# Attention rows: x and kv transposed by DMA blocks and DVE instead of TensorE, group norm folded into two weights, v and the variances on ScalarE

## The chip, the cores and the metric

The kernel runs on one core of a Trainium2 chip. Its time is that of one execution on the device in microseconds (us). A core has TensorE (PE; PEld is its weight load), VectorE (DVE), ScalarE (ACT), GpSimd (POOL) and the DMA engines; SyncE (SP) issues most of the DMAs. SBUF is the on-chip memory, PSUM the memory that PE writes to, in banks of 512 floats per partition.

## The reference, cut to what matters

Two layers are added to x, of shape (1, 256, 256, 128). The change lies in layer 0: attention along each of the 256 rows, with 4 heads of 32 channels, on a group-normalised x.

```python
# layer 0: x = x + L0(_gn(x), kv_x, ...)      _gn: 32 groups of 4 channels over the whole image, eps 1e-5
q = split_heads(einsum('...qi,oi->...qo', q_x, wq)) / sqrt(32)
k = split_heads(einsum('...ki,oi->...ko', kv_x, wk))
v = split_heads(einsum('...ki,oi->...ko', kv_x, wv))
a = softmax(einsum('bshqd,bshkd->bshqk', q, k) + bias1 + bias2, axis=-1)
o = einsum('bshqk,bshkd->bshqd', a, v)
g = sigmoid(einsum('...qi,oi->...qo', q_x, wg) + bg)
out = einsum('...qi,oi->...qo', o * g, wo) + bo
# layer 1: x = x + L1(_gn(x), ...)   tokens = channels; instance norms, small Fourier modes, mixing
```

bias1 is (head, query, key) and the same for all rows; bias2 is (row, key). Everything is float32.

## The kernel before, in words

`layer0` first streams the whole of x for the group statistics (xb, L135 to L140), meanwhile turns the weights, and ends with the mean and the scale of each channel (mr, nmr). `Rows.prepare` makes exp(bias1), scaled, with keys on partitions (b1T), and bias2 with keys on partitions (b2T).

Then `Rows.run` goes over the 256 rows, one row of 256 tokens by 128 channels an iteration. The order on PE, ACT, DVE and POOL is the order in which the code is written (`tc.manual_schedule`); only SP's order is left to the scheduler. Each engine works through its own list and waits where an input or a buffer is not ready. Iteration i holds the steps of several rows:

- `load` (L242, every second iteration): x and kv of two rows, tokens on partitions, two neighbouring tokens to a partition.
- `scores(i)` (L305): eight matmuls of 32 channels, into two PSUM tiles of two banks each, s0 and s1, with one buffer each. Then three of the four exps on ACT (L314), with bias2 as the bias column: those of heads 0 and 1 stay in PSUM (sc), those of heads 2 and 3 go to e1 in SBUF.
- `project(i+1)`: q and k (L279, L280), copied by ACT to qkT (L282); v and the gate (L285, L289), v copied by DVE (L291), the gate through tanh on ACT (L293). The fourth exp of row i follows.
- `turn(i+2)`: four 128x128 transposes of x and kv on PE (L268, L269), then two ACT steps to SBUF: the group norm applied to x (xnT, L271) and a copy of kv (kvT, L273).
- `weigh(i)`: DVE multiplies heads 0 and 1 by b1T out of PSUM (e0, L327), POOL heads 2 and 3 in SBUF (e1, L332); then POOL adds the two key halves of each pair of heads (es, L336, twice), which is half of the softmax's sum.
- `out(i-3)`: the output projection (L366), the sum with x1 on DVE (L370), the store to x1d.
- `spectrum(i-4)`: x1 turned on PE (L379) and its Fourier sums over the row (L381); DVE takes bn_stats of the turned row (L384), ACT copies the sums (L385).
- `attend(i-1)`: e times v and the sums of es over keys, both into one bank (L344, L349); DVE: og = (gate + 1) times that (L355), a reciprocal of the sums (L356), their product (L357); POOL: x + bo (L360).

PSUM tiles other than the scores share one pool of four banks under tag "a", taken in turn: qk, gv, tr, wo, u, av each iteration. A step that takes a bank waits for the readers of the tile that had it four tiles earlier.

A few one-time steps stand in DVE's list: in iterations 8 to 15 a reduce over b1T each (L413), in iteration 16 five tiny steps on the results (L419 to L423), and every 32 rows `gather`, which sums up the bn_stats. They decide whether the biases are small enough; if not, `layer0_general` does the rows again, which does not happen with these inputs.

Of the kernel before, what the change touches and what calls it, by code (L numbers as in the profile page):

```python
# [18 lines left out]
P = 128  # L19
# [50 lines left out]
class Groups:  # L70
# [13 lines left out]
    def make(self, pool, psum, mv2, tag):  # L84

        nc = self.nc
        mv = pool.tile([P, 2], FP, name=tag + "mv")
        dv = pool.tile([P, 8], FP, name=tag + "dv")
        nc.vector.tensor_reduce(mv[:, 0:1], mv2[:, :, 0], AX.X, ALU.add)
        nc.vector.tensor_scalar(mv[:, 0:1], mv[:, 0:1], 0.125, None, ALU.mult)  # L90
        nc.vector.tensor_scalar(dv, mv2[:, :, 0], mv[:, 0:1], None, ALU.subtract)
        nc.vector.tensor_mul(dv, dv, dv)
        nc.vector.tensor_add(dv, dv, mv2[:, :, 1])
        nc.vector.tensor_reduce(mv[:, 1:2], dv, AX.X, ALU.add)
        nc.vector.tensor_scalar(mv[:, 1:2], mv[:, 1:2], 0.125, None, ALU.mult)
        nc.vector.tensor_copy(self.mr, group_stats(nc, pool, psum, mv, self.gavg, tag))
        nc.vector.tensor_scalar(self.bdft, self.raw, self.mr[:, 1:2], None, ALU.mult)


def layer0(tc, I, C, ident, x1d, U, stats2, mv2, groups):  # L100
# [11 lines left out]
    with ExitStack() as ctx:  # L112
# [4 lines left out]
        nmr = const.tile([P, 1], FP, name="nmr1")  # L117
        bg = const.tile([P, 1], FP, name="bg")

        bad = const.tile([P, 3, 8], FP, name="bad")  # L120
# [4 lines left out]
        rows = Rows(tc, I, rctx, x1d, U, stats2, mv2, wT, mr, nmr, bg, adft, bad, ident)  # L125
        with tc.tile_pool(name="l0p", bufs=2) as pp, tc.tile_pool(
# [6 lines left out]
            for b in range(xr.shape[0]):  # L133
# [7 lines left out]
                if b == 2:  # L141
                    nc.sync.dma_start(gavg, C["gavg"])
                    nc.sync.dma_start(bg, I["L0_conv_bg"].unsqueeze(1))
                    nc.sync.dma_start(adft, C["adft"].rearrange("(p j) f -> p j f", j=2))
# [18 lines left out]
            nc.vector.tensor_scalar(nmr, mr[:, 0:1], mr[:, 1:2], -1.0, ALU.mult, ALU.mult)  # L163
# [4 lines left out]
        with tc.tile_pool(name="l0f", bufs=1) as fp, tc.tile_pool(  # L168
# [5 lines left out]
            nc.vector.tensor_scalar(z, bad[:, 2, :], 0.0, None, ALU.mult)  # L174
# [12 lines left out]
            with tc.If(again > 0):  # L187
                layer0_general(tc, I, ident, x1d, U, stats2, wT, mr, bg, adft)
                for k in range(8):
                    nc.vector.bn_aggr(mv2[:, k, :], stats2[:, 32 * k : 32 * k + 32, :].rearrange("p a b -> p (a b)"))  # L190
                groups.make(fp, ps_g, mv2, "g3")


class Rows:
# [6 lines left out]
    def __init__(self, tc, I, ctx, x1d, U, stats2, mv2, wT, mr, nmr, bg, adft, bad, ident):  # L201
        self.tc, self.I, self.ctx, self.x1d, self.U, self.stats2 = tc, I, ctx, x1d, U, stats2
        self.wT, self.mr, self.nmr, self.bg, self.adft = wT, mr, nmr, bg, adft
# [4 lines left out]
        self.ld = ctx.enter_context(tc.tile_pool(name="l0ld", bufs=2))  # L208
        self.hbg = const.tile([P, 1], FP, name="hbg")
        self.bo = const.tile([P, P], FP, name="bo")  # L210
# [5 lines left out]

    def prepare(self, bp, ps_b):
        nc, I, ident = self.tc.nc, self.I, self.ident
        nc.gpsimd.memset(self.ones, 1.0)
        nc.scalar.mul(self.hbg, self.bg, 0.5)  # L220
# [3 lines left out]
        nc.sync.dma_start(b1n, I["L0_conv_bias1"][0, 0].rearrange("h (p j) k -> p h j k", j=2))  # L224
        b2n = bp.tile([P, 2, 256], FP, name="b2n", bufs=1)
        nc.sync.dma_start(b2n, I["L0_conv_bias2"][0, :, 0, 0, :].rearrange("(j p) k -> p j k", p=P))
        for h in range(4):
            ps = ps_b.tile([P, 512], FP, tag="a", name=f"b1ps_{h}")
            for c in range(2):
                for j in range(2):  # L230
                    nc.tensor.transpose(
                        ps[:, (2 * c + j) * P : (2 * c + j + 1) * P], b1n[:, h, j, c::2], ident
                    )
# [4 lines left out]
        for c in range(2):  # L238
            for j in range(2):
                nc.tensor.transpose(  # L240
                    ps[:, (2 * c + j) * P : (2 * c + j + 1) * P], b2n[:, j, c::2], ident
# [3 lines left out]
    def load(self, g):  # L245
        nc, SG = self.tc.nc, self.SG
        s0 = g * SG
        xt = self.ld.tile([P, SG, 2, P], FP, tag="xt", name=f"xt_{g}", bufs=4)
        nc.sync.dma_start(xt, self.x[s0 : s0 + SG].rearrange("s (p j) c -> p s j c", j=2))
        kt = self.ld.tile([P, SG, 2, P], FP, tag="kt", name=f"kt_{g}")  # L250
        nc.sync.dma_start(kt, self.kv[s0 : s0 + SG].rearrange("s (p j) c -> p s j c", j=2))
        for i in range(SG):
            self.rows[s0 + i] = {"x": xt[:, i], "kv": kt[:, i]}

    def run(self):
# [8 lines left out]
        def turn(s):  # L264
            r = rows[s]
            ps = ps_a.tile([P, 512], FP, tag="a", name=f"tr_{s}")
            for j in range(2):
                nc.tensor.transpose(ps[:, j * P : (j + 1) * P], r["x"][:, j, :], ident)  # L268
                nc.tensor.transpose(ps[:, 256 + j * P : 256 + (j + 1) * P], r["kv"][:, j, :], ident)  # L269
            r["xnT"] = wk.tile([P, 256], FP, tag="xnT", name=f"xnT_{s}")  # L270
            nc.scalar.activation(r["xnT"], ps[:, 0:256], AF.Identity, bias=self.nmr, scale=self.mr[:, 1:2])  # L271
            r["kvT"] = wk.tile([P, 256], FP, tag="kvT", name=f"kvT_{s}")
            nc.scalar.copy(r["kvT"], ps[:, 256:512])  # L273

        def project(s):
            r = rows[s]
            xnT, kvT = r["xnT"], r["kvT"]
            ps = ps_a.tile([P, 512], FP, tag="a", name=f"qk_{s}")
            nc.tensor.matmul(ps[:, 0:256], wT["wq"], xnT, start=True, stop=True)  # L279
            nc.tensor.matmul(ps[:, 256:512], wT["wk"], kvT, start=True, stop=True)  # L280
            r["qkT"] = wk.tile([P, 512], FP, tag="qkT", name=f"qkT_{s}")
            nc.scalar.copy(r["qkT"], ps)  # L282
# [6 lines left out]
            nc.tensor.matmul(ps[:, 0:256], wT["wg"], xnT, start=True, stop=True)  # L289
            r["v"] = wk.tile([P, 2, P], FP, tag="v", name=f"v_{s}", bufs=3)  # L290
            nc.vector.tensor_copy(r["v"].rearrange("p c d -> p (c d)"), ps[:, 256:512])  # L291
            r["gate"] = wk.tile([P, 256], FP, tag="gate", name=f"gate_{s}", bufs=3)
            nc.scalar.activation(r["gate"], ps[:, 0:256], AF.Tanh, bias=self.hbg, scale=0.5)  # L293
            if s > 0:
                rows[s - 1].pop("exp")(1, 1)

        def scores(s):
# [22 lines left out]
            exp(1, 0)  # L320
# [3 lines left out]
        def weigh(s):  # L324
# [9 lines left out]
            for hp in (1, 0):  # L334
                e = r["e"][hp]
                nc.gpsimd.tensor_tensor(r["es"][hp], e[:, :, 0, :], e[:, :, 1, :], ALU.add)  # L336
# [25 lines left out]
        def out(s):  # L362
# [10 lines left out]
            nc.sync.dma_start(self.x1d[s].rearrange("(p j) c -> p j c", j=2), r["x1"])  # L373

        def spectrum(s):
# [8 lines left out]
            nc.vector.bn_stats(self.stats2[:, s, :], ps[:, 0:256])  # L384
            nc.scalar.copy(self.U[:, :, s], ps[:, 256 : 256 + 129])  # L385

        def gather(k):


            st = self.stats2[:, 32 * k : 32 * k + 32, :].rearrange("p a b -> p (a b)")  # L390
            nc.vector.bn_aggr(self.mv2[:, k, :], st)
            nc.vector.tensor_reduce(bad[:, 2, k : k + 1], st, AX.X, ALU.add)

        with tc.manual_schedule(engines={ENG.PE, ENG.Activation, ENG.DVE, ENG.Pool}):
            turn(0)
            turn(1)
            project(0)
            for i in range(NS + 4):
                if i % SG == 0 and i // SG + 2 < NS // SG:
                    self.load(i // SG + 2)  # L400
                if i < NS:
                    scores(i)
                if i + 1 < NS:
                    project(i + 1)
                elif i < NS:
                    rows[i].pop("exp")(1, 1)
                if i + 2 < NS:
                    turn(i + 2)
                if i < NS:
                    weigh(i)  # L410
# [13 lines left out]
                if i % 32 == 7 and i > 32:  # L424
                    gather(i // 32 - 1)
# [7 lines left out]
            gather(7)  # L433


def layer0_general(tc, I, ident, x1d, U, stats2, wT, mr, bg, adft):
# [4 lines left out]
    with ExitStack() as ctx:  # L441
# [5 lines left out]
        nc.sync.dma_start(b1, I["L0_conv_bias1"][0, 0].rearrange("h (p j) k -> p h j k", j=2))  # L447
# [4 lines left out]
        with tc.For_i(0, NS, 1) as s:  # L452
            one = bass.ds(s, 1)
            xt = wk.tile([P, 2, P], FP, name="g_xt")
            nc.sync.dma_start(xt, x[one].rearrange("s (p j) c -> p (s j) c", j=2))
# [78 lines left out]
            nc.sync.dma_start(x1d[one].rearrange("s (p j) c -> p (s j) c", j=2), x1)  # L534
# [7 lines left out]
            nc.vector.bn_stats(stats2[:, one, :].rearrange("p o k -> p (o k)"), ps[:, 0:256])  # L542
# [3 lines left out]
def layer1(tc, I, C, ident, x1d, upool, U, stats2, groups, out):  # L546
# [1547 lines left out]
```

## Time and profile before

| | |
|---|---|
| timed runs | 2865.82, 2868.55, 2876.69 us; median 2868.55 |
| profiled execution, first to last instruction (the only time the page has of it) | 2861.4 us |
| PE busy | 2629.8 us, 92% |
| DVE busy | 2008.6 us, 70% |
| POOL busy | 1668.0 us, 58% |
| ACT busy | 1488.9 us, 52% |
| statistics of x | until about 108 us |
| attention rows | about 110 to 1652 us |
| layer 1 | the rest |
| DMA packets | 245121, 424.35 MB |
| granted clock of PE, mean | 0.958 (1.00 in the rows) |

The profile is one execution. Busy time is that of instructions that do work, not of waits. In a list by time each line is a start in us, a length in us, the engine, the line of the kernel, the operation, output<-inputs by the program's tile names, the shape and how many instructions were merged; square brackets hold the idle time before it and what ended that. In the table of stretches, busy time of each engine (and its instructions) is followed by PE's granted clock, the DMA engines' mean busy share and GB/s.

### The profile page before, as it was taken

How to read it: one execution, taken by the hardware profiler on the slowest of the kernel's cores; microseconds unless marked ns; L12 is line 12 of the kernel's file. 1: busy time of each engine (PE TensorE's matmuls, PEld its weight loads, DVE VectorE, ACT ScalarE, POOL GpSimd, SP SyncE). 2: the span in 40 equal slices, each digit the busy share in tenths (PEclk: the TensorE clock that was granted, in tenths of full speed). 3: DMA queues.
4: the chain of work that ended last, by engine and by line, in shares of the span. 5: the costliest groups of instructions: out<-in, count | busy, mean ns of one | idle time of the engine just before them, and what ended most of it. 6: DMA issues, size and time to landing. Idle time of an engine off the chain costs nothing. (4 is left out here: it accounts for less than half of the span.)

```text
span 2861.4 us, 71473 instructions
## 1 busy us (share of the span) xinstructions
PE 2629.8 (92%) x29116; PEld 1922.9 (67%) x29116; DVE 2008.6 (70%) x3274; ACT 1488.9 (52%) x2847; POOL 1668.0 (58%) x1298
## 2 busy tenths in 40 slices
PE   6799999999999999999999989999897988789655
PEld 6677777777777777777777755778675555545433
DVE  7788888888888888888888853756664656356445
ACT  0477777777777777777777721310103621355132
POOL 0399999999999999999999900300214632111211
PEclk9999999999999999999999999999998999899855
DMA  9422222222222222222222101088887784898599
GB/s 367 171 68 68 68 68 67 67 68 68 68 68 68 68 68 68 67 65 65 65 66 68 53 28 54 1 272 274 291 296 266 253 301 141 278 350 303 189 357 345
DMA packets 245121, 424.35 MB, mean 148 GB/s; under 512 B 26102, under 2 KB 174025, under 8 KB 238392
## 3 DMA queue, kind: packets, MB, share of 16 engines
q1 hardware_dynamic: 204984, 329.57, 34.7%
q0 software_dynamic: 22912, 81.80, 7.4%
q10 hardware_dynamic: 16896, 8.39, 1.0%
q8 instruction: 231, 3.78, 0.6%
q14 instruction: 98, 0.80, 0.1%
HBM read 284.40 MB, written 135.27 MB: 147 GB/s over the span
## 5 line engine op out<-in xcount | busy, mean ns | idle before, releaser
L332 POOL TENSOR_TENSOR e<-e,b1T 128x1024 f32<-128x1024 f32 x256 | 606.7, 2370 | 163.7 <-PE u L381 88.8
L336 POOL TENSOR_TENSOR es<-e 128x512 f32<-128x512 f32 x512 | 639.9, 1271 | 20.1
L314 ACT ACTIVATE sc<-sc,b2T 128x512 f32<-128x512 f32 x512 | 339.0, 662 | 364.6 <-PE sc L305 356.3
L356 DVE RECIPROCAL av<-av 128x256 f32<-128x256 f32 x256 | 452.3, 1767 | 27.2 <-DVE og L355 1.4
L314 ACT ACTIVATE e<-sc,b2T 128x512 f32<-128x512 f32 x512 | 348.7, 681 | 0.0
L327 DVE TENSOR_TENSOR e<-sc,b1T 128x1024 f32<-128x1024 f32 x256 | 311.1, 1215 | 0.0
L305 PE MATMUL sc<-qkT 32*128 32x256 f32 x4096 | 293.4, 400 | 1.3 <-DVE e L327 1.3
L344 PE MATMUL av<-e,v 128*32 128x256 f32 x4096 | 274.7, 385 | 0.5 <-POOL e L332 0.5
L1352 PE MATMUL yps<-xt,mpT 128*128 128x256 f32 x1024 | 247.4, 392 | 28.3 <-DVE yt L1364 14.4
L305 PEld LDWEIGHTS sc<-qkT 32*128 32x128 f32 x4096 | 185.1, 184 | 112.3 <-issue 97.8
L355 DVE SCALAR_TENSOR_TENSOR og<-gate,av 128x256 f32<-128x256 f32 x256 | 107.8, 421 | 190.6 <-PE av L349 190.6
L1352 PEld LDWEIGHTS yps<-xt,mpT 128*128 128x128 f32 x1024 | 192.6, 193 | 72.7 <-DVE yt L1364 19.9
L1368 POOL DMA_DIRECT2D yd<-yt x32 | 17.5, 546 | 314.6 <-DVE yt L1364 311.9
L360 POOL TENSOR_TENSOR x<-xt,bo 128x256 f32<-128x256 f32 x256 | 188.1, 735 | 0.0
L279 PE MATMUL qk<-xnT,wT_wq 128*128 128x256 f32 x512 | 179.5, 432 | 1.7 <-ACT xnT L271 1.7
L285 PEld LDWEIGHTS gv<-wT_wv,kvT 128*128 128x128 f32 x1024 | 155.0, 192 | 13.4
L349 PE MATMUL av<-es,ones 128*32 128x256 f32 x2048 | 157.5, 379 | 2.6 <-POOL es L336 2.5
L366 PE MATMUL wo<-wT_wo,og 128*128 128x128 f32 x1024 | 156.8, 276 | 2.7 <-DVE og L357 2.7
L344 PEld LDWEIGHTS av<-e,v 128*32 128x32 f32 x4096 | 107.0, 109 | 76.1 <-POOL e L332 1.0
L381 PE MATMUL u<-adft,x 128*128 128x129 f32 x1024 | 156.4, 275 | 0.0
L291 DVE COPY v<-gv 128x256 f32<-128x256 f32 x256 | 108.7, 425 | 67.5 <-PE gv L289 67.5
L285 PE MATMUL gv<-wT_wv,kvT 128*128 128x128 f32 x1024 | 156.0, 275 | 0.0
(543 smaller groups left out, 5228.5 us busy)
## 6 DMA issues: line engine op xcount, KB each, us to landing
xt<-x1d SPq DMA_DIRECT2D x128, 512.0 KB, 6.7
xb<-in_x_dram SPq DMA_DIRECT2D x32, 1024.0 KB, 7.8
xt<-in_x_dram SPq DMA_DIRECT2D x128, 256.0 KB, 2.7
kt<-in_L_conv_kv_x_dram SPq DMA_DIRECT2D x128, 256.0 KB
x1d<-x SPq DMA_DIRECT2D x256, 128.0 KB, 2.6
y<-yd SPq DMA_DIRECT2D x62, 512.0 KB, 7.3
gs<-Gd SPq DMA_DIRECT2D x384, 64.0 KB, 5.4
yd<-yt POOLq DMA_DIRECT2D x32, 512.0 KB, 6.2
```

The costliest lines, as they stand in the source:

```text
L279: nc.tensor.matmul(ps[:, 0:256], wT["wq"], xnT, start=True, stop=True)
L285: nc.tensor.matmul(ps[:, 256 + c * P : 256 + (c + 1) * P], kvT[:, c * P : (c + 1) * P], wT["wv"], start=True, stop=True,)
L305: nc.tensor.matmul(sc[h // 2][:, h % 2, c * 256 : (c + 1) * 256], qkT[p, 256 + c * P : 256 + (c + 1) * P], qkT[p, 0:256], start=True, stop ...
L314: nc.scalar.activation(r["e"][1][:, :, c, :] if hp else z, z, AF.Exp, bias=b2T[:, c, s : s + 1])
L327: nc.vector.tensor_tensor(r["e"][0].rearrange("p h c q -> p (h c q)"), r.pop("sc").rearrange("p h x -> p (h x)"), b1T[:, 0:2].rearrange("p ...
L332: nc.gpsimd.tensor_tensor(e1, e1, b1T[:, 2:4].rearrange("p h c q -> p (h c q)"), ALU.mult)
L336: nc.gpsimd.tensor_tensor(r["es"][hp], e[:, :, 0, :], e[:, :, 1, :], ALU.add)
L344: nc.tensor.matmul(ps[hd, 0:256], r["v"][:, c, hd], r["e"][h // 2][:, h % 2, c, :], start=(c == 0), stop=(c == 1),)
L349: nc.tensor.matmul(ps[32 * h : 32 * h + 32, 256:512], self.ones, r["es"][h // 2][:, h % 2, :], start=True, stop=True,)
L356: nc.vector.reciprocal(rd, rd)
L360: nc.gpsimd.tensor_tensor(r["x1"], r["x"], bc(self.bo, 1, 2), ALU.add)
L1352: nc.tensor.matmul(rows_of(ps[j]), mpT[:, sc, tt], by_turn(xt[:, sc])[:, j], start=(sc == 0), stop=False,)
```

## The change

In the rows, PE no longer turns x and kv. `load` brings each row twice over: once in blocks, so that partition 32a + t holds channels 32a to 32a+31 of the tokens t, 32 + t, 64 + t and so on, by eight DMAs for two rows (four blocks of channels for x, four for kv), in pieces of 32 floats; and, in the new `load_x`, x with tokens on partitions for the residual. `turn` is one DVE instruction that transposes all 32x32 blocks of x and kv of a row (xkT). The group norm is no longer applied to x: `fold` multiplies wq and wg by the scale once and turns the mean into bias columns (qb for q, hbg for the gate), so qkT becomes an ACT step with a bias. ACT takes over v's copy from DVE, and the row's sum of squares (Square with an accumulator, into Q2) replaces bn_stats; the row sums come from U. The last two exps move behind qkT (`rest`), `weigh` goes ahead of `turn`, and of heads 0 and 1 the es add of head 0 goes to DVE, that of head 1 stays on POOL as a half, ahead of the es add of heads 2 and 3. Tokens 0 to 127 and 128 to 255 of a row now form the two halves where neighbouring tokens were paired, in every layout that depends on it. The PSUM pool has no tr tile any more.

```diff
+def row_sums(nc, U, Q2, mv2, k):
+    t = slice(32 * k, 32 * k + 32)
+    nc.vector.tensor_reduce(mv2[:, k, 0:1], U[:, 0, t], AX.X, ALU.add)
+    nc.vector.tensor_reduce(mv2[:, k, 1:2], Q2[:, t], AX.X, ALU.add)
...
+    def fold(self, psum, mr):
+        nc = self.tc.nc
+        nc.vector.tensor_scalar(self.nm, mr[:, 0:1], -1.0, None, ALU.mult)
+        ps = psum.tile([P, 512], FP, tag="a", name="foldps")
+        for k, n in enumerate(("wq", "wg")):
+            nc.vector.tensor_scalar(self.wn[n], self.wT[n], mr[:, 1:2], None, ALU.mult)
+            nc.tensor.matmul(ps[:, k : k + 1], self.wn[n], self.nm, start=True, stop=True)
+        nc.vector.tensor_copy(self.qb, ps[:, 0:1])
+        nc.vector.tensor_scalar(self.hbg, ps[:, 1:2], self.bg, 0.5, ALU.add, ALU.mult)
...
     def load(self, g):
-        xt = self.ld.tile([P, SG, 2, P], FP, tag="xt", name=f"xt_{g}", bufs=4)
-        nc.sync.dma_start(xt, self.x[s0 : s0 + SG].rearrange("s (p j) c -> p s j c", j=2))
-        kt = self.ld.tile([P, SG, 2, P], FP, tag="kt", name=f"kt_{g}")
-        nc.sync.dma_start(kt, self.kv[s0 : s0 + SG].rearrange("s (p j) c -> p s j c", j=2))
+        t = self.ld.tile([P, 2, 8 * SG, 32], FP, tag="xk", name=f"xk_{g}")
+        for k, src in enumerate((self.x, self.kv)):
+            blocks = src[rs].rearrange("s (b t) c -> t (s b) c", t=32)
+            for a in range(4):
+                ch = slice(32 * a, 32 * a + 32)
+                nc.sync.dma_start(t[ch, k], blocks[:, :, ch])
...
+    def load_x(self, g):
+        xt = self.ld.tile([P, SG, 2, P], FP, tag="xt", name=f"xt_{g}", bufs=2)
+        nc.sync.dma_start(xt, self.x[g * SG : (g + 1) * SG].rearrange("s (j p) c -> p s j c", p=P))
...
         def turn(s):
-            ps = ps_a.tile([P, 512], FP, tag="a", name=f"tr_{s}")
-            for j in range(2):
-                nc.tensor.transpose(ps[:, j * P : (j + 1) * P], r["x"][:, j, :], ident)
-                nc.tensor.transpose(ps[:, 256 + j * P : 256 + (j + 1) * P], r["kv"][:, j, :], ident)
-            nc.scalar.activation(r["xnT"], ps[:, 0:256], AF.Identity, bias=self.nmr, scale=self.mr[:, 1:2])
-            nc.scalar.copy(r["kvT"], ps[:, 256:512])
+            r["xkT"] = wk.tile([P, 512], FP, tag="xkT", name=f"xkT_{s}")
+            nc.vector.transpose(r["xkT"].rearrange("p (k n) -> p k n", k=2), r.pop("xk").rearrange("p k b c -> p k (b c)"))
...
         def project(s):
-            nc.scalar.copy(r["qkT"], ps)
+            nc.scalar.activation(r["qkT"], ps, AF.Identity, bias=self.qb)
+            if s > 0:
+                rest(s - 1)
...
-            nc.vector.tensor_copy(r["v"].rearrange("p c d -> p (c d)"), ps[:, 256:512])
+            nc.scalar.copy(r["v"].rearrange("p c d -> p (c d)"), ps[:, 256:512])
...
-            if s > 0:
-                rows[s - 1].pop("exp")(1, 1)
+        def rest(s):
+            exp = rows[s].pop("exp")
+            exp(1, 0)
+            exp(1, 1)
...
         def weigh(s):
-            for hp in (1, 0):
-                e = r["e"][hp]
-                nc.gpsimd.tensor_tensor(r["es"][hp], e[:, :, 0, :], e[:, :, 1, :], ALU.add)
+            e = r["e"][0]
+            nc.vector.tensor_tensor(r["es"][0][:, 0], e[:, 0, 0], e[:, 0, 1], ALU.add)
+            nc.gpsimd.tensor_tensor(r["es"][0][:, 1], e[:, 1, 0], e[:, 1, 1], ALU.add)
+            e = r["e"][1]
+            nc.gpsimd.tensor_tensor(r["es"][1], e[:, :, 0, :], e[:, :, 1, :], ALU.add)
...
         def spectrum(s):
-            nc.vector.bn_stats(self.stats2[:, s, :], ps[:, 0:256])
+            nc.scalar.activation(
+                ps[:, 0:256], ps[:, 0:256], AF.Square, accum_out=self.Q2[:, s : s + 1]
+            )
...
             for i in range(NS + 4):
+                if i % SG == 1 and i // SG + 1 < NS // SG:
+                    self.load_x(i // SG + 1)
...
+                if i < NS:
+                    weigh(i)
                 if i + 2 < NS:
                     turn(i + 2)
-                if i < NS:
-                    weigh(i)
```

Layer 1's first steps read the row sums in U and Q2 where they read the fields of bn_stats before; a few small DVE steps fall away there.

## The prediction

> **What bounds the kernel now.** I read the page's busy shares first, then the busy table of a stretch in the attention rows, then the order in time inside one row, then the waits.
>
> ```profile
> PE 2629.8 (92%) x29116; PEld 1922.9 (67%) x29116; DVE 2008.6 (70%) x3274; ACT 1488.9 (52%) x2847; POOL 1668.0 (58%) x1298
> ```
>
> ```profile
> 1000.00:1200.00 200.00, 200.00 (x2127) 152.46 (x2127) 162.56 (x237) 149.86 (x301) 185.70 (x134) 1.00 0.21 66
> ```
>
> The second fence is the busy table of 200 us of the row loop (columns PE, PEld, DVE, ACT, POOL, granted clock, DMA share, GB/s). PE has no idle time, at full clock; POOL is at 93%, DVE 81%, ACT 75%; DMA is at 21%. The row loop runs from about 110 to 1650 us; the change lives there.
>
> ```profile
> 1004.64 1.15 PE L305 MATMUL sc<-qkT 32*128 32x256 f32 x16
> 1004.78 0.42 DVE L355 SCALAR_TENSOR_TENSOR og<-gate,av 128x256 f32<-128x256 f32 x1 [0.79 <-PE av L349]
> 1005.30 1.77 DVE L356 RECIPROCAL av<-av 128x256 f32<-128x256 f32 x1
> 1005.88 1.36 ACT L314 ACTIVATE sc<-sc,b2T 128x512 f32<-128x512 f32 x2 [1.47 <-PE sc L305]
> 1007.11 0.42 DVE L357 SCALAR_TENSOR_TENSOR og<-av,og 128x256 f32<-128x256 f32 x1
> 1007.16 0.68 ACT L314 ACTIVATE e<-sc,b2T 128x512 f32<-128x512 f32 x1
> 1007.56 0.27 PE L268 MATMUL tr<-ident,xt 128*128 128x128 f32 x1
> ...
> 1007.73 0.59 ACT L282 COPY qkT<-qk 128x512 f32<-128x512 f32 x1
> ...
> 1008.00 0.61 PE L366 MATMUL wo<-wT_wo,og 128*128 128x128 f32 x4
> 1008.11 1.22 DVE L327 TENSOR_TENSOR e<-sc,b1T 128x1024 f32<-128x1024 f32 x1
> ...
> 1008.45 0.38 PE L379 MATMUL u<-ident,x 128*128 128x128 f32 x2
> 1009.36 2.37 POOL L332 TENSOR_TENSOR e<-e,b1T 128x1024 f32<-128x1024 f32 x1 [0.35 <-PE u L381]
> ...
> 1010.64 1.15 PE L305 MATMUL sc<-qkT 32*128 32x256 f32 x16
> ```
>
> One row, scores to scores, is 1010.64 - 1004.64 = 6.00 us, and PE's starts follow each other without a wait. DVE and ACT wait for PE each row (0.79 and 1.47 us). So today a row is PE's issue time.
>
> **What is removed.** The four transposes of x and kv (L268, L269) hold PE from 1007.56 to 1008.00: 0.44 us. Nothing replaces them on PE, so PE's row becomes 5.56 us. Over about 254 rows that is -112 us, if PE still sets the pace.
>
> **The other engines, busy time per row** (33.3 rows in the 200 us). ACT is 149.86/33.3 = 4.50; it loses xnT 0.57 and kvT 0.38, gains the v copy (kvT's row, 0.38), a Square with accumulator (nearest row L1080, 0.50) and about 0.08 because qkT becomes an ACTIVATE with a bias column (L314 steps 0.57, the COPY 0.49): 4.5. POOL is 5.57; one es add of 1.27 shrinks to half, 0.61 to 0.86 (128x256 adds of L1417): about 5.0. DVE is 4.88; it loses the v copy and bn_stats (0.42 each), gains a 128x256 add (0.42, L370's size) and the 32x32 transpose of 128x512, which no row shows. A COPY of 128x512 from PSUM is 0.69 (L939), from SBUF 0.58 (L769); POOL's slower 128x512 add, 1.27, is my upper bound. I take 0.69, the same size on the same engine: DVE 5.15. All stay under 5.56, so on counts alone the change wins.
>
> The Trainium skill, "VectorE: DVE Perf Modes", section "The three transpose paths", gives 311 ns for a 128x128 transpose on this engine; four of them would be 1.24 us (an estimate), and no run here shows one. By that figure DVE's round worked out below would be 5.74 instead of 5.19 and the blocked rhythm 6.73 us a row.
>
> **Transfers.** Per two rows x and kv come as 8 DMAs of 512 packets of 128 B, plus one x load and two stores in 512 B packets: 4096 + 1024 packets. The row "q10 hardware_dynamic: 16896, 8.39, 1.0%" gives 0.010 x 2861 x 16 / 16896 = 27 ns for a packet of about 500 B. At that price 5120 x 27 / 16 = 8.6 us per two rows, under 11.1; smaller packets should not cost more. At the stretch's 1 KB price (0.204 x 200 x 16 / 13587 = 48 ns) the 128 B ones alone would take 12.3. I take the first: hidden. SP issues 11 DMAs instead of 4 per two rows, 0.4 us each by its rows, 4.6 us of 11.1; in the changed program's order a row's blocks are issued beside the store of the row ten earlier, some four rows ahead of their use, so a landing of 2.7 us is covered. If that cover goes, DVE's transpose waits and all of DVE's row queues behind it.
>
> **The wait that the change adds.** The new es half on DVE is a tensor_tensor with both inputs in SBUF, and POOL is nearly always inside a tensor_tensor. No DVE step of the row loop before is of that kind (each has an input in PSUM), but a one-time step of row 16 is:
>
> ```profile
> 210.06 2.37 POOL L332 TENSOR_TENSOR e<-e,b1T 128x1024 f32<-128x1024 f32 x1 [0.36 <-PE u L381]
> ...
> 210.19 0.15 DVE L422 TENSOR_SCALAR bad<-bad 128x1 f32<-128x1 f32 x1
> 210.38 2.06 DVE L423 TENSOR_TENSOR bad<-bad 128x1 f32<-128x1 f32 x1
> ```
>
> The second view is that of one line of layer 1 (min, median and max in ns):
>
> ```profile
> L1103 DVE SCALAR_TENSOR_TENSOR mT<-pT,hq,mT x7: 744/1482/1487, 1792.7 to 1848.4; 128x512 f32<-128x512 f32 x7
> ```
>
> L423 multiplies two columns, normally 0.15 us, and took until 212.44, the end of POOL's instruction (212.43). L1103, also all SBUF, doubles in the same way when POOL is first. So the price of the new add is 0.42, or the rest of POOL's instruction and then some 0.2.
>
> The Trainium skill says so as a rule against such a change ("SBUF — State Buffer", section "Who interferes with whom"): the DVE instruction with two SBUF inputs and a GpSimd instruction that reads SBUF exclude each other for a whole instruction. By the rule the sum is the one by the row; it also leaves the transpose free if that runs in no two-port mode, which nothing here shows.
>
> So the question is which comes first in a row, counted from the start of scores. POOL's e1 multiply starts after the fourth exp: 1.24 (scores to first exp) + 1.28 (two exps) + 0.57 (qkT, now ahead of the last two) + 0.58 + 0.68 + 0.08 = 4.43. DVE: og at 0.14, reciprocal 0.66, og2 2.47, e0 multiply 2.81, done 4.02, add asked for at 4.06. POOL's previous work ends near 3.8. The add slips in, 0.37 us ahead of e1. DVE's round is then 0.525 + 1.80 + 0.34 + 1.25 + 0.34 + 0.60 + 0.33 = 5.19 (starts to next starts; transpose 0.69 less 0.09 overlap), 0.37 less than PE's 5.56; on every second row seven DMA waits ahead of the transpose may take 0.25 of that.
>
> But rows 8 to 15 carry an extra reduce of 0.676 on DVE (L413; 0.60 in a queue). DVE's round becomes 5.79, 0.23 over PE's, more on the even rows. After two rows the 0.37 is used up, the add finds e1 running and waits to its end at 4.43 + 2.33 = 6.76. Behind it on DVE queue the transpose, the x1 add, og, reciprocal and og2; og2 frees the PSUM bank that the u transposes of the next row on PE need. That closes a loop of two rows: 6.76 + 0.22 (add) + 0.60 + 0.33 + 0.525 + 1.80 + 0.425 + 0.07 (signal), then on PE from u to the next scores 0.76 + 0.89 + 0.55 = 2.20. Sum 12.93 us, **6.46 us per row**. In this rhythm the add is asked for about 0.9 us inside a 2.37 us multiply, so a small jitter does not end it. With a transpose of 0.58 or 1.27 the row is 6.40 or 6.75.
>
> **Small edits.** fold adds a few 0.15 to 0.23 us steps and two matmuls before the first row, layer 1's start loses as many, the moment sums replace bn_aggr: within 2 us together. Plain halves instead of interleaved rows alter no count of work on the engines.
>
> **Sum.** Span 2861.4 us; the median of the runs is 2868.55, 7.1 more, which I keep. About 246 rows at +0.46 = +113, the first eight at -0.44 = -4, rows 8 to 17 some +3 more: 2868.6 + 112 = 2980.
>
> **Rivals.**
> (1) *PE keeps the pace*: the add keeps slipping in ahead of e1 (margin 0.37), or a shift in row 16 restores that order. For it: the counts, PE's unbroken issue. Against it: rows 8 to 15. 2868.6 - 112 = 2757; with 0.02 us a row lost either way 2750 to 2790. It decides as long as DVE lags PE by less than that margin. Chance 0.33.
> (2) *Transfers set the pace*: if a 128 B packet cost the 48 ns of a 1 KB one, two rows need 12.3 + 1.7 (1024 of 27 ns) = 14.0 us, 7.0 a row, +256 us: 3125. It decides from about 36 ns a packet on, where two rows reach 11.1. Against it: the 27 ns row. 0.05.
> (3) *A mix*: stretches of both rhythms, or a multiply that misses by less: 2800 to 2950; a part of this is no change. 0.08.
> (4) *The change does not do what it says*: the transposes stay on DVE at over 1.27 us; then DVE's round is past 5.8 without any lock and the lock only adds: above 3050. 0.05.
> The forecast, add behind e1, 0.49 with its own range 2945 to 3050.
>
> Two in ten may lie outside, so the range must take in both rhythms: 2750 to 3050. Half a per cent, 14 us, is about what a measurement of this kernel tells from no change. Slower by over that: forecast 0.49, transfers 0.05, slow transpose 0.05, a third of the mix 0.03, in all 0.62. Faster: rival 1 with 0.33 and a little of the mix, 0.34. Same: 0.04.
>
> **What would show it.** The es add on DVE near 1.5 to 2.5 us mean instead of 0.42; scores starting 6.4 to 6.5 us apart after row 10 and 5.56 before row 8; PE idle before u, released by DVE; POOL idle before e1. I am wrong if the es add stays near 0.42 (rival 1 then), if DVE waits for xk landings (rival 2), or if the transpose's own row is far from 0.69.

## The result, and the profile after

The changed kernel takes 2984.49 us, the median of four runs (2983.48 to 2993.75), against 2868.74 us before: 1.0405 times as long, 95% interval 1.0383 to 1.0427. The forecast was 2980. The size is right; part of that is luck, because two terms of the sum were off in opposite directions, and the experiments show which.

The profiled execution has a span of 2992.0 us and is the longest of the four. From the page, the busy shares, and from the costliest groups three lines (busy time, mean ns of one, idle time ahead of them and what ended it):

```profile
PE 2581.1 (86%) x28096; PEld 1840.0 (61%) x28096; DVE 2339.2 (78%) x3270; ACT 1524.4 (51%) x3102; POOL 1550.9 (52%) x1298
...
L358 POOL TENSOR_TENSOR e<-e,b1T 128x1024 f32<-128x1024 f32 x256 | 607.6, 2373 | 410.6 <-ACT e L341 332.8
...
L361 DVE TENSOR_TENSOR es<-e 128x256 f32<-128x256 f32 x256 | 396.3, 1548 | 8.7
...
L300 PE MATMUL qk<-xkT,wn_wq 128*128 128x256 f32 x512 | 179.1, 431 | 107.8 <-DVE x L398 102.1
```

The new es add (L361) takes 1.548 us in the mean, where a step of its size is 0.42. POOL, at 93% in the rows before, now sits idle 411 us ahead of its multiply, 333 of them for ACT, and PE, which had no idle time in the rows before, is idle 108 us ahead of q, 102 of them for DVE.

The busy table shows that the rows have two rhythms (columns as before: PE, PEld, DVE, ACT, POOL, granted clock, DMA share, GB/s):

```profile
300.00:500.00 200.00, 200.00 (x2164) 150.18 (x2160) 183.72 (x255) 161.55 (x361) 178.94 (x145) 1.00 0.48 97
1000.00:1200.00 200.00, 173.17 (x1790) 125.09 (x1782) 194.90 (x211) 138.58 (x298) 153.62 (x120) 1.00 0.38 79
```

In the first stretch PE is busy throughout and a row takes 5.56 us, what the prediction gave for a PE without transposes. In the second DVE is at 97%, PE at 87%, and a row takes 6.73. The clock is full in both. Going by the starts of the es add, rows 4 to 17 take 6.74 us in the mean, rows 18 to 79 take 5.56 each (the last 5.91), and rows 80 to 255 take 6.72. The add is longer than 1 us in 190 of the 256 rows.

One blocked row, in order of time:

```profile
1005.83 2.38 POOL L358 TENSOR_TENSOR e<-e,b1T 128x1024 f32<-128x1024 f32 x1 [1.58 <-ACT e L341]
...
1006.51 1.98 DVE L361 TENSOR_TENSOR es<-e 128x256 f32<-128x256 f32 x1
...
1008.41 0.70 DVE L294 STREAM_TRANSPOSE xkT<-xk 128x512 f32<-128x512 f32 x1
...
1009.04 0.38 DVE L398 TENSOR_TENSOR x<-wo,x 128x256 f32<-128x256 f32 x1
...
1009.48 0.70 PE L300 MATMUL qk<-xkT,wn_wq 128*128 128x256 f32 x2 [0.62 <-DVE x L398]
...
1010.64 0.69 ACT L304 ACTIVATE qkT<-qk,qb 128x512 f32<-128x512 f32 x1 [0.40 <-PE qk L301]
...
1011.23 1.26 ACT L341 ACTIVATE e<-sc,b2T 128x512 f32<-128x512 f32 x2
...
1012.57 2.38 POOL L358 TENSOR_TENSOR e<-e,b1T 128x1024 f32<-128x1024 f32 x1 [1.58 <-ACT e L341]
...
1013.24 1.98 DVE L361 TENSOR_TENSOR es<-e 128x256 f32<-128x256 f32 x1
```

The add is asked for 0.68 us after POOL's multiply has started and ends 0.28 after it (1008.49 against 1008.21). Behind it on DVE wait the transpose and the x1 add (L398), to 1009.42; PE's q and k of the next row start 0.06 after the x1 add's end, qkT 1.16 after that, the two exps 0.59 later and last 1.26, and 0.08 on POOL multiplies again. 2.38 + 0.28 + 0.93 + 0.06 + 1.16 + 0.59 + 1.26 + 0.08 = 6.74: a loop of one row. It lasts because from the end of a late add the next multiply is only 4.08 us away (0.93 + 0.06 + 1.16 + 0.59 + 1.26 + 0.08), while DVE's own list reaches the next add after 4.75: in the median of the 175 rows, as here, the multiply is again 0.67 ahead. The waits of 900 to 1100 us say the same (us in total, times, longest):

```profile
POOL e L358 <- ACT e L341: 47.2, 30, 1.6
PEld qk L300 <- DVE x L398: 29.1, 29, 1.0
...
PE u L407 <- DVE og L385: 9.3, 30, 0.7
```

The third line is the wait that the prediction named. It is there, but 0.3 us a row; the loop closes earlier, at q.

### The profile page after: what moved, and what is told of

Same layout as the page of the kernel before. It is cut to its first block, busy times and chain, and to the rows that moved or that the text cites. A ratio compares the mean times of both kernels' runs of the same rounds, so it can differ in the third digit from the quotient of the medians.

```text
span 2992.0 us, 70856 instructions
## 1 busy us (share of the span) xinstructions
PE 2581.1 (86%) x28096; PEld 1840.0 (61%) x28096; DVE 2339.2 (78%) x3270; ACT 1524.4 (51%) x3102; POOL 1550.9 (52%) x1298
## 5 line engine op out<-in xcount | busy, mean ns | idle before, releaser
L361 DVE TENSOR_TENSOR es<-e 128x256 f32<-128x256 f32 x256 | 396.3, 1548 | 8.7
L364 POOL TENSOR_TENSOR es<-e 128x512 f32<-128x512 f32 x256 | 324.2, 1266 | 0.0
L353 DVE TENSOR_TENSOR e<-sc,b1T 128x1024 f32<-128x1024 f32 x256 | 311.0, 1215 | 8.4 <-PE gv L313 6.8
L300 PE MATMUL qk<-xkT,wn_wq 128*128 128x256 f32 x512 | 179.1, 431 | 107.8 <-DVE x L398 102.1
L362 POOL TENSOR_TENSOR es<-e 128x256 f32<-128x256 f32 x256 | 220.6, 862 | 0.0
L304 ACT ACTIVATE qkT<-qk,qb 128x512 f32<-128x512 f32 x256 | 175.5, 685 | 72.3 <-PE qk L301 71.5
L300 PEld LDWEIGHTS qk<-xkT,wn_wq 128*128 128x128 f32 x512 | 76.3, 188 | 204.9 <-DVE x L398 170.4
L294 DVE STREAM_TRANSPOSE xkT<-xk 128x512 f32<-128x512 f32 x256 | 179.1, 700 | 0.3 <-DMA xk<-in_L_conv_kv_x_dram 0.2
L394 PEld LDWEIGHTS wo<-wT_wo,og 128*128 128x128 f32 x1024 | 154.3, 191 | 16.2 <-DVE og L385 1.6
L309 PEld LDWEIGHTS gv<-wT_wv,xkT 128*128 128x128 f32 x1024 | 154.7, 192 | 14.3 <-DVE x L398 0.7
L407 PE MATMUL u<-ident,x 128*128 128x128 f32 x512 | 103.0, 283 | 67.5 <-DVE og L385 65.2
```

The source lines that it names most:

```text
L300: nc.tensor.matmul(ps[:, 0:256], self.wn["wq"], xT, start=True, stop=True)
L353: nc.vector.tensor_tensor(r["e"][0].rearrange("p h c q -> p (h c q)"), r.pop("sc").rearrange("p h x -> p (h x)"), b1T[:, 0:2].rearrange("p ...
L361: nc.vector.tensor_tensor(r["es"][0][:, 0], e[:, 0, 0], e[:, 0, 1], ALU.add)
L362: nc.gpsimd.tensor_tensor(r["es"][0][:, 1], e[:, 1, 0], e[:, 1, 1], ALU.add)
L364: nc.gpsimd.tensor_tensor(r["es"][1], e[:, :, 0, :], e[:, :, 1, :], ALU.add)
```

## The experiments

Times before, on the chips of the three groups of runs: 2870.43, 2871.68 and 2873.29 us. Ratios are to these.

**Is it the exclusion, and is it this one step?** Two kernels take it away in different manners.

```diff
 es_on_pool
-            nc.vector.tensor_tensor(r["es"][0][:, 0], e[:, 0, 0], e[:, 0, 1], ALU.add)
-            nc.gpsimd.tensor_tensor(r["es"][0][:, 1], e[:, 1, 0], e[:, 1, 1], ALU.add)
+            nc.gpsimd.tensor_tensor(r["es"][0], e[:, :, 0, :], e[:, :, 1, :], ALU.add)
```

> The es add of head 0 goes back to POOL (one 128x512 add for heads 0 and 1), all else as changed. Lock theory: no DVE step of the row loop has two SBUF inputs any more, so nothing on DVE waits for POOL's multiply; DVE's round is about 4.8, PE needs 5.56, and POOL has 2.37 + 1.27 + 1.27 + 0.73 = 5.64 us a row, so POOL sets the pace at about 5.65 from the first row on and the time is about 2868.6 - 0.35 x 250 = 2780 (2765 to 2800). Rival, transfers: the 128 B packets set the pace or slow every engine; then the row stays above 6.4 and the time near 2980. Rival, DVE transposes: their own work is what is too long; then only 0.42 us a row is saved and the time is near 2880.

Measured: 2773.97 us, ratio 0.9666 (0.9637 to 0.9694). From row 17 on the rows are 5.56 us, counted from reciprocal to reciprocal (twice 5.9 and then 5.25). POOL did not set the pace: its steps overlap a little, and it is busy 198.6 us in the stretch from 1000 to 1200 at PE's 5.56.

```diff
 psum_input
-            nc.vector.tensor_tensor(r["es"][0][:, 0], e[:, 0, 0], e[:, 0, 1], ALU.add)
+            nc.vector.tensor_tensor(r["es"][0][:, 0], r.pop("sc")[:, 0, 0:256], e[:, 0, 1], ALU.add)
```

> The es add on DVE stays, same size and same place, but its first input is read from the PSUM tile of the scores instead of e0 in SBUF, so its sums are not those of the reference. Lock theory: only a step with both inputs in SBUF is excluded, so the add is 0.42 to 0.45 us in every row, PE keeps 5.56 us a row throughout, and the time is 2757 to 2775. Rival, too much work on DVE: the same instruction count and size leaves the row at 6.73 in most rows and the time near 2980. Rival, transfers: near 2980 too.

Measured: 2767.9 us, ratio 0.9644 (0.9599 to 0.969). Here DVE does the same number of instructions of the same size at the same places. The view of the add's line (min, median and max in ns):

```profile
L361 DVE TENSOR_TENSOR es<-sc,e x256: 424/425/426, 121.6 to 1538.1; 128x256 f32<-128x256 f32 x128
```

It is never late in 256 rows. So neither DVE's load nor the transfers lengthen the rows; the whole loss in them hangs on this add having both inputs in SBUF. The Trainium skill says in "SBUF — State Buffer", section "Who interferes with whom", that a DVE instruction with at most one input in SBUF does not contend with GpSimd, the modes that use both of its ports left aside; the trace agrees, with 424 to 426 ns.

**Is the loop the one read from the blocked row?**

```diff
 turn_first
+            if s + 2 < NS:
+                turn(s + 2)
             nc.vector.tensor_tensor(r["es"][0][:, 0], e[:, 0, 0], e[:, 0, 1], ALU.add)
...
-                if i + 2 < NS:
-                    turn(i + 2)
```

> The DVE transpose is moved ahead of the es add on DVE; nothing else. Lock theory: the add is asked for about 0.63 us later, after POOL's e1 has started in every row (the margin in the unblocked rows is 0.32), so the rows are blocked throughout; but the loop of the blocked rows (multiply 2.38, rest of the add 0.28, transpose and x1 add 0.93, signal 0.05, q and k 1.17, qkT 0.59, two exps 1.26, signal 0.08: 6.74) loses the transpose: about 6.1 us a row and 2868.6 + 0.12 x 250 = 2900 (2880 to 2920), with no row at 5.56. If the loop runs through og2 and the PSUM bank of u instead, as the prediction had it, 12.93 - 0.63 = 12.3 for two rows, 6.15: about 2905, not to be told apart by the time but by who releases qk and u in the trace. Rival, a fixed cost of the new DVE steps: no change, 2985.

Measured: 2933.05 us, ratio 1.022 (1.0181 to 1.0259); from row 18 on rows of 6.14 and 6.25 us in turn, none at 5.56. One of the 6.14 (the x1 add is L400 here):

```profile
1003.40 2.38 POOL L358 TENSOR_TENSOR e<-e,b1T 128x1024 f32<-128x1024 f32 x1 [1.10 <-ACT e L341]
...
1003.84 0.70 DVE L294 STREAM_TRANSPOSE xkT<-xk 128x512 f32<-128x512 f32 x1
...
1004.47 1.58 DVE L363 TENSOR_TENSOR es<-e 128x256 f32<-128x256 f32 x1
...
1005.97 0.41 DVE L400 TENSOR_TENSOR x<-wo,x 128x256 f32<-128x256 f32 x1
...
1006.44 0.70 PE L300 MATMUL qk<-xkT,wn_wq 128*128 128x256 f32 x2
...
1007.62 0.68 ACT L304 ACTIVATE qkT<-qk,qb 128x512 f32<-128x512 f32 x1
1007.83 0.72 POOL L390 TENSOR_TENSOR x<-xt,bo 128x256 f32<-128x256 f32 x1
...
1008.19 1.27 ACT L341 ACTIVATE e<-sc,b2T 128x512 f32<-128x512 f32 x2
...
1009.54 2.37 POOL L358 TENSOR_TENSOR e<-e,b1T 128x1024 f32<-128x1024 f32 x1 [0.99 <-ACT e L341]
```

The same chain without the transpose: 6.14 from multiply to multiply, against 6.1 expected. The transpose ends at 1004.54, and q still starts 0.06 after the x1 add (1006.38): it is the x1 add that lets q go, and the transpose had only stood in the line ahead of it. Why q waits for the x1 add is not shown. In the other rows qkT starts 1.29 us after q instead of 1.18, because ACT is still in the first two exps of the row (until 1001.56 in the row at 1000). Those exps follow the scores, and the scores follow u, which waits 0.3 us for og2 in every row here: so the prediction's path binds too once the transpose is out of the line. The 6.25 us rows are some 13 us of the 33 above the expected 2900; in this trace layer 1 is also 20 us longer than before (1228.7 against 1208.5), of which more below. The margin fits too: with the add 0.63 later it is late in every row from row 18 on (in rows 6 to 17 in every second one).

**Two rhythms, and what tips the rows from one to the other.** In the changed kernel's trace the free rows end here:

```profile
576.63 0.42 DVE L361 TENSOR_TENSOR es<-e 128x256 f32<-128x256 f32 x1
...
576.95 2.37 POOL L358 TENSOR_TENSOR e<-e,b1T 128x1024 f32<-128x1024 f32 x1 [0.59 <-ACT e L341]
...
578.27 0.42 DVE L383 SCALAR_TENSOR_TENSOR og<-gate,av 128x256 f32<-128x256 f32 x1 [0.29 <-PE av L377]
...
579.15 1.77 DVE L384 RECIPROCAL av<-av 128x256 f32<-128x256 f32 x1 [0.46 <-DVE og L383]
...
581.29 1.21 DVE L353 TENSOR_TENSOR e<-sc,b1T 128x1024 f32<-128x1024 f32 x1
...
582.51 2.36 POOL L358 TENSOR_TENSOR e<-e,b1T 128x1024 f32<-128x1024 f32 x1 [0.59 <-ACT e L341]
582.54 2.61 DVE L361 TENSOR_TENSOR es<-e 128x256 f32<-128x256 f32 x1
```

In a free row the add starts 0.32 us ahead of the multiply. The reciprocal at 579.15 comes 0.455 after og, not 0.103 as in the other rows. The 0.35 (0.36 in the expectations, from rounded times) is more than the margin; the next add is 0.03 late and waits for the whole multiply, and the loop above keeps it so for all 176 rows from this add on. Number DVE's records from 0, with those of its sequencer (the waits for semaphores) counted. Then such a reciprocal always stands at place 63 modulo 128 (places 1087, 1215 and 2751 here, 575 and 703 in es_on_pool), and no reciprocal at another place of the rows does it. That can be tested by adding work.

```diff
 pad2 (pad18: 18 for 2)
         nc.vector.memset(onec, 1.0)
+        pad = const.tile([P, 2], FP, name="pad")
+        for k in range(2):
+            nc.vector.memset(pad[:, k : k + 1], 0.0)
```

> Two memsets of one column each are put at the head of DVE's list, long before the first row; nothing else. In the traces so far a reciprocal that stands at place 63 modulo 128 among DVE's records starts 0.46 us after og instead of 0.10 (rows 78, 89 and 222 of the changed kernel; rows 37 and 49 with es on POOL), and in the changed kernel the blocked rows begin at row 78. Theory: that stall of 0.36 us is more than the add's margin of 0.32 and is what tips the rows into the blocked rhythm. Shifted by two places, no reciprocal after row 17 stands at such a place, so the rows stay at 5.56 us from row 18 to the end: 176 rows x 1.17 = 206 us less, about 2780 (2770 to 2800). If the shift comes out as one or three places, the first stall is at row 111 or 100, and the time 2945 or 2960. Rival, the rows are tipped at that time by something else (a transfer, a drift): near 2985, tipped near row 78.

> The control: eighteen such memsets instead of two. Shifted by 18 places, a reciprocal stands at place 63 modulo 128 in row 21 already, four rows after the rows have come free. Theory: blocked again from row 21 on, 57 more rows at 1.17 us: about 2984.5 + 67 = 3050. Rival, as above: near 2985. If it is only the presence of added steps that helps, it is faster, as the other one.

Measured: pad2 2790.49 us, ratio 0.9717 (0.9693 to 0.974); pad18 3049.29 us, ratio 1.0618 (1.0597 to 1.0639). The line of the add in pad2, then in pad18 (L364 in both):

```profile
L364 DVE TENSOR_TENSOR es<-e x256: 424/426/2372, 121.1 to 1552.8; 128x256 f32<-128x256 f32 x128
```

```profile
L364 DVE TENSOR_TENSOR es<-e x256: 425/1975/2591, 121.6 to 1817.9; 128x256 f32<-128x256 f32 x128
```

The median add is free in one and waits for the multiply in the other. Two memsets outside the loop save 194 us, eighteen cost 65; between the two lie 259 us, and nothing in the rows differs. In pad2 the rows are free from row 18 to the end, but for the last add. Twice there the e0 multiply, at places 1855 and 1983 (63 modulo 128 too), starts 0.17 us late; the add still comes 0.14 ahead of POOL's multiply, and the rows stay free. In pad18 the reciprocal of row 21 is stalled, and the first late add after row 17 is that of row 23, which follows it in DVE's list. The cause of the tipping is settled: the stall, by its place in DVE's list.

```diff
 nudge
+            for _ in range(3 if s % 16 == 12 else 1):
                 nc.gpsimd.tensor_tensor(r["es"][1], e[:, :, 0, :], e[:, :, 1, :], ALU.add)
```

> In every sixteenth row (12, 28, 44 and so on) POOL does its es add of heads 2 and 3 three times instead of once, with the same result: 2.5 us more work on POOL in 16 of 256 rows. Theory: POOL's next multiply then starts about 1 us late, behind the add of DVE, which is asked for only 0.68 us after that start in a blocked row, so that one late start frees all rows up to the next stall. Blocked rows: 4 to 13, 78 to 93 and 222 to 237, some 40 instead of 190: about 2985 - 150 x 1.17 = 2810 (2790 to 2850); more work on POOL, and 6 per cent faster. Rival, no two rhythms but a lasting cost (transfers, DVE's own work): 2985 or up to 40 us more.

Measured: 2835.63 us, ratio 0.9874 (0.9854 to 0.9894). POOL does more, and it is 149 us faster than the changed kernel. After row 28 all rows are 5.56 but for one of 6.46 at each added step, and two stretches of 13 late adds at about 6.7: from the stalls of the reciprocals of rows 78 and 222 to the next step that frees them. The step of row 12 did not free the rows, which the expected 2810 had counted on: it puts off the next multiply to 203.65, and the add, asked for at 203.84, is still behind it. Nor did they come free at row 16, so they stayed blocked up to the step of row 28.

**The trigger that the prediction had named, and the split alone.**

```diff
 bias_only
             project(0)
+            (the eight reduces and the five steps on bad, in the same form)
             for i in range(NS + 4):
...
-                if 8 <= i < 16:
...
-                if i == 16:
```

> The changed kernel with the eight reduces of rows 8 to 15 and the five small steps of row 16 ahead of the row loop, and POOL's order left as changed. The prediction held the reduces to be what tips the rows; in the changed kernel's trace the add is late from row 4 on already, and the rows come free in row 16, where one of the five steps is itself kept waiting by POOL and lets DVE fall behind a whole multiply. If the start of the rows tips them (theory now): late from about row 4 and never free again, all but a few rows at 6.73 us: 118 + 252 x 6.73 + 1225 = 3039, so about 3040 (3025 to 3060), slower by 55 for taking work out of the rows. If the reduces are what tips them (the prediction): 5.56 us up to row 77, blocked after row 78 as before: 14 x 1.2 less, about 2968. If the later start of the first row (by up to 5 us) lets the add in ahead from the beginning, also about 2968.

Measured: 2975.16 us, ratio 1.0353 (1.0317 to 1.0389); rows of 5.56 from row 5 on, tipped after the stall at row 78, then 6.73 to the end. That was my second case, not the one that I held likelier: here the start of the rows did not tip them. In the changed kernel row 4 is a tie, the add asked for at 143.249 and the multiply started at 143.269, and POOL went first; in bias_only the same two stand at 139.373 and 139.397, and DVE went first. In pad18, where the adds of rows 2 to 9 take under 1 us, the next late add is in row 10, after the reduces of rows 8 and 9. So the reduces can tip the rows, as predicted, and in the changed kernel's trace a tie in row 4 did it before the first reduce.

```diff
 split_only (the kernel before, with)
-            for hp in (1, 0):
-                e = r["e"][hp]
-                nc.gpsimd.tensor_tensor(r["es"][hp], e[:, :, 0, :], e[:, :, 1, :], ALU.add)
+            e = r["e"][0]
+            nc.vector.tensor_tensor(r["es"][0][:, 0], e[:, 0, 0], e[:, 0, 1], ALU.add)
+            nc.gpsimd.tensor_tensor(r["es"][0][:, 1], e[:, 1, 0], e[:, 1, 1], ALU.add)
+            e = r["e"][1]
+            nc.gpsimd.tensor_tensor(r["es"][1], e[:, :, 0, :], e[:, :, 1, :], ALU.add)
```

> The kernel before, with only the es split of the change (head 0's half on DVE, head 1's half on POOL, ahead of the es add of heads 2 and 3). In the kernel before, e0 ends at 1009.33 and POOL's e1 multiply starts at 1009.36, so the add is asked for just as e1 starts. Lock theory: it loses at once or after the first small stall, and then waits in most rows; DVE, with 4.88 + 0.42 us of work, falls behind until its wait in a row is down to what the row leaves, and og and og2 come later by some 1.1 us than PE needs them: 6.0 to 6.6 us a row, most likely 6.3: 2868.6 + 0.3 x 250 = 2945 (2868 to 3020), the add's mean over 1 us. Rival, the loss comes from the transposes, the loads or the order of the exps: no change from before, 2865 to 2875, with the add at 0.42.

Measured: 2889.37 us, ratio 1.0064 (1.003 to 1.0099), far less than my 2945. Eight of the 256 adds are late; a late add (2.5 to 2.6 us) makes one row 7.73 and the next 5.80, from reciprocal to reciprocal, and then the rows are at 6.00 again. One late add and what follows:

```profile
487.18 2.36 POOL L332 TENSOR_TENSOR e<-e,b1T 128x1024 f32<-128x1024 f32 x1 [0.75 <-ACT e L314]
487.28 2.54 DVE L335 TENSOR_TENSOR es<-e 128x256 f32<-128x256 f32 x1
...
493.06 0.41 DVE L291 COPY v<-gv 128x256 f32<-128x256 f32 x1
...
493.50 0.47 ACT L293 ACTIVATE gate<-gv,hbg 128x256 f32<-128x256 f32 x1 [0.33 <-DVE v L291]
...
494.63 2.66 POOL L332 TENSOR_TENSOR e<-e,b1T 128x1024 f32<-128x1024 f32 x1 [2.32 <-ACT e L314]
494.64 0.42 DVE L335 TENSOR_TENSOR es<-e 128x256 f32<-128x256 f32 x1
```

In this order too the multiply hangs on the late add, by a longer way: through DVE's list to v's copy, then the gate and the fourth exp on ACT. So the multiply is put off as far as the add is. After all eight late adds the next multiply and the next add start together, both 4.81 to 4.82 us after the late add's end (5.94 in one case), and the add gets in; in the changed kernel it was 4.08 against 4.75. Here the lock costs what one wait costs. Three parts of the change alter these two ways: the last exps go ahead of the gate, behind qkT; v's copy goes to ACT; the transpose stands on DVE. turn_first, with the transpose ahead of the add, stays blocked from row 18 on too; apart from that they were not tested one by one.

**A version that keeps the gain.**

```diff
 half_first (early_bias: this, and bias_only's edit)
-            e1 = r["e"][1].rearrange("p h c q -> p (h c q)")
-            nc.gpsimd.tensor_tensor(e1, e1, b1T[:, 2:4].rearrange("p h c q -> p (h c q)"), ALU.mult)
             r["es"] = [...]
             e = r["e"][0]
             nc.vector.tensor_tensor(r["es"][0][:, 0], e[:, 0, 0], e[:, 0, 1], ALU.add)
             nc.gpsimd.tensor_tensor(r["es"][0][:, 1], e[:, 1, 0], e[:, 1, 1], ALU.add)
+            e1 = r["e"][1].rearrange("p h c q -> p (h c q)")
+            nc.gpsimd.tensor_tensor(e1, e1, b1T[:, 2:4].rearrange("p h c q -> p (h c q)"), ALU.mult)
```

> POOL's half of the es add of heads 0 and 1 is moved ahead of its e1 multiply; nothing else. Both halves wait for the same e0, so DVE's add can meet only the 0.72 us half and never the 2.37 us multiply. Lock theory: if the add goes first each time the row is 5.56 us (2757 to 2765); if POOL's half goes first each time, DVE's round is 5.19 + 0.52 = 5.71 (about 2795). So 2755 to 2800, with no long blocked stretch. Rival, that any of the other new steps holds the rows up: near 2980.

> half_first, with the eight reduces of rows 8 to 15 and the five small steps of row 16 moved ahead of the row loop on DVE, where DVE waits some 6.8 us for the first scores. In half_first rows 6 to 13 take 5.80 and 5.77 us instead of 5.56 and row 14 7.49, together 3.8 us; these should go: the stage of the rows from 1431.7 to about 1428 us, and the time from 2771 to 2767, less than these runs tell apart by the total, so the stage is what is to be read. If the reduces do not fit into the wait, the first row starts later by up to 5 us.

Measured: half_first 2771.27 us, ratio 0.9653 (0.9621 to 0.9686); early_bias 2766.82 us, ratio 0.9639 (0.9618 to 0.966). Both are faster than the kernel before and the changed one. POOL's short half now waits for the same e0 as DVE's add, and the multiply stands behind that half, so it comes after the add however late DVE is. The add's line in half_first (min, median and max in ns):

```profile
L359 DVE TENSOR_TENSOR es<-e x256: 424/426/1015, 121.5 to 1540.7; 128x256 f32<-128x256 f32 x128
```

Its longest wait is that of row 1, and the multiply starts at least 0.97 after the add in all 256 rows. The three stalls are still there (rows of 5.91), and the row after each takes 5.25: the time is made up. From the first scores to the last reciprocal early_bias takes 1427.4 us, half_first 1431.7, the changed kernel 1648.5 and the kernel before 1540.4; the 4 us between the first two are the 3.8 expected, and the totals don't tell them apart.

## Why the prediction was right, and where it was wrong

- **PE at 5.56 without the transposes: right.** It is the row of every free stretch, to 0.01 us.
- **Engines' counts: right.** In psum_input's stretch of 36 rows ACT is 161.54/36 = 4.49 (predicted 4.5), POOL 178.96/36 = 4.97 (5.0) and DVE 183.64/36 = 5.10 (5.15). With a reduce in the row DVE's round is 5.81 and 5.77 in turn there (5.79); so the DMA waits of every second row cost some 0.04, not the 0.25 that was allowed for them. The transpose is 0.70 (0.69), between 0.67 and 0.71 in all 256 rows of the changed kernel, in the free rows beside POOL's multiply: the exclusion does not touch it. The 1.24 that I had worked out from the Trainium skill's figure for a 128x128 transpose ("VectorE: DVE Perf Modes", "The three transpose paths"; there the figure is for bf16) is not what this chip does for 128x512 floats: the measurement decides. That the prediction's 6.73 us a row by that figure is also the blocked row measured is chance.
- **The exclusion, the add behind the multiply: right,** with a margin of 0.32 (predicted 0.37) and an end 0.28 after the multiply (0.22). psum_input and es_on_pool show that it is the whole loss.
- **The loop: the wrong one.** The step that failed is "That closes a loop of two rows", 12.93 us, by og2 and the bank of u. I had listed the transpose and the x1 add behind the es add and not asked who waits for them before og2 comes: q and k of the next row, which start 0.06 after the x1 add. With the exps moved behind qkT, the multiply itself hangs on the add of the row before, and before DVE is back at the next add. That loop is 6.73 a row, 0.27 more than my 6.46, and turn_first shortened it by 0.59 (to 6.14), about the 0.63 that the transpose holds up DVE.
- **How many rows are blocked: wrong.** "About 246 rows at +0.46 = +113" became 14 rows at +0.74, 62 at -0.44 and 175 at +0.72, that is 10 - 27 + 126 = +109 (the stage of the rows measures +108.1). Two errors cancelled; what happened is closer to my rival of a mix, with a higher price, than to the forecast's single rhythm.
- **"so a small jitter does not end it": right for the blocked rhythm,** which lasts from row 80 to the end. What I did not ask is what jitter does to the other one. The margin is 0.32, not 0.37, and one stall of 0.35 us ends it; so rival 1's 2757 was not to be had with this list of DVE's steps, though two memsets ahead of it were enough to keep 237 adds in time.
- **The trigger:** rows 8 to 15 can tip the rows (pad18), but in this trace a tie in row 4 came first. That a shift in row 16 frees them, which rival 1 mentions, did happen: L449 was kept waiting by POOL, and the add then came at the end of the multiply.
- **Transfers: hidden, as taken.** In the blocked stretch 77901 packets of queue q1 take 37.9% of 16 engines in 200 us, 15.6 ns each, against the 27 that I used; even the free rows take only 0.48 of the DMA engines' time.
- **Small edits "within 2 us": too little.** The first scores start at 118.3 instead of 112.5 (at 114.4 to 116.8 in the variants of the changed kernel). With the rows' 108.1 this gives 113.9 of the 115.7 us between the medians. The profiled execution has 16.7 us more than that of before in layer 1 as well (1225.1 against 1208.5), but this differs from execution to execution: it is 1216 to 1231 us in the traces of the variants, and 1217.5 in split_only, whose layer 1 is that of the kernel before. The longer ones have the lower granted clock there, 0.89 in the changed kernel and pad2, 0.90 in split_only and nudge, 0.91 before. What the change itself does to layer 1 stays open.

## What to carry to other kernels

Where two engines exclude each other, the price of a new step is not its wait but what stands behind it. Follow two ways from the end of a late step: to the other engine's next long step, and to the next request of the late step itself. If the first is shorter (4.08 against 4.75 us here), one late start lasts; if they are equal (4.81 and 4.82 in split_only), it costs one wait. Compare the margin with the longest stall that the trace shows anywhere, not with zero. And make the order certain through a shared input or the order on the long step's engine, instead of counting on who is first.

## What the runs showed of the hardware that I had not expected

A reciprocal of 128x256 that stands at place 63 modulo 128 among DVE's records, counted as above, starts 0.35 us later than the others. From the third row on this was so in every such case in the traces of the kernel before (places 575, 1087 and 1983), the changed one and all variants, and pad2 and pad18 moved it as counted. Other steps at such places start late in some cases only (the e0 multiply by 0.17 in pad2). What happens at these places is not shown. The Trainium skill ("Runtime: NRT & Kernel Launch", "Instruction fetch mechanics") speaks of blocks of 256 instructions whose fetch is mostly hidden; the distance here is 128 records, and the 0.35 us are not hidden. I do not claim that it is the fetch.

The loser of the exclusion does not always get in at the next boundary. In es_on_pool a product of two columns (normally 0.15 us) waited through the rest of the multiply and three more POOL steps that followed without a gap, until POOL fell idle; the row took 10.1 us. DVE's line, then POOL's:

```profile
209.06 5.07 DVE L448 TENSOR_TENSOR bad<-bad 128x1 f32<-128x1 f32 x1
```

```profile
208.57 2.42 POOL L358 TENSOR_TENSOR e<-e,b1T 128x1024 f32<-128x1024 f32 x1
210.90 1.32 POOL L361 TENSOR_TENSOR es<-e 128x512 f32<-128x512 f32 x1
212.12 1.32 POOL L363 TENSOR_TENSOR es<-e 128x512 f32<-128x512 f32 x1
213.34 0.78 POOL L387 TENSOR_TENSOR x<-xt,bo 128x256 f32<-128x256 f32 x1
```

In the blocked rows the add got in at the end of the multiply with another POOL step following, so what decides this stays open. Nor do the recorded starts tell who wins a tie: in split_only a multiply at 1002.26 was held up (2.66 us) by an add at 1002.27, and in the tie of row 4 the same recorded order ended one way in bias_only and the other in the changed kernel.
